# Convolution kernels of seven head groups: sum over n moved from TensorE to VectorE

## The chip, the cores and the metric

The kernel runs on one core of a Trainium2 chip. The metric is the device time of one launch in microseconds (us). Three runs of the kernel before gave 977.91, 977.95 and 978.32 us, so the median is 977.95 us. Of the core's engines this text uses TensorE (PE in the profile; its weight loads are the row PEld), VectorE (DVE), ScalarE (ACT), GpSimd (POOL) and the DMA queue that SyncE issues (SP).

## The reference

The input `x` has 64 batch entries, 64 heads h and 1024 positions l. Two layers are applied. The first is a masked long convolution with one kernel for each head, and the second a gated low-rank expert layer that is added to `x`:

```
A = -exp(log_A_real) + 1j*A_imag            # 64 heads x 64 n
dtA = A * exp(log_dt)
Cs = Cc * (exp(dtA) - 1) / A
K = 2 * real( sum over n of Cs[h,n] * exp(dtA[h,n] * l) )     # 64 x 1024
y = (causal convolution of x*mask with K) + x*mask*D[h],  times mask
scores = y @ Wr.T;  top 16 of 64 -> softmax -> gates G
out = x + 2 * einsum( (y @ A_experts) * G, B_experts )
```

What is changed here is one step in the first layer: how the sum over n is taken for the first 128 positions of K.

## The kernel before

**Groups.** The 64 heads are worked on in 8 groups of 8 heads (`HG`), a group being 4 pairs of heads (`GP`). The positions are cut into 8 blocks of 128 (`P`). For each group the generator `tables(g)` makes the tables of the convolution, `conv(g, ...)` computes `y` of the group, `gates(g, y)` the gates, and `first(g, ...)` the first half of the expert layer (`h` products, line L553, in a seven-product scheme for 2x2 blocks). When all groups are done, `second(...)` computes the other half (`s` products, L1042), from about 582 us on.

**Interleaving.** These pieces are generators. A group's `h` products are laid between the convolution steps of the next group and the table steps of the group after that, so that TensorE always has something to do. The order on each engine is made by a scheduler when the program is built; it orders by its own estimates wherever the code doesn't pin the order. Each engine then runs its instructions strictly in that order. An instruction whose input is late holds all that stands behind it on its engine.

**Tables of a group.** From `mag`, `sn`, `sh` comes `w` (L355, powers of exp(dtA) for 129 positions). For each pair i a table `b` of 128 partitions (2 heads x 64 n) by 128 positions is made twice: `b[:, 0, :]` is the real part, whose sum over n is the kernel K, and `b[:, 1, :]` the other part. Both are turned by TensorE (`transpose`, L326, into the PSUM tile `pb`) and copied by ScalarE to `bt` (L330). So `bt[:, i, P:]` holds the turned real part: positions on partitions, 2 heads x 64 n along the row. `bt` is the stationary operand of `pu` (L618), which makes the states `s` that are carried from block to block (`recur`, L366).

**The first chunk of K.** `kernels` (L285 and on) sums over n on TensorE: `heads` is a 128x2 constant with ones for each head's 64 rows, and `pk` = heads^T times `b[:, :, 0, :]` (L293), two matrix multiplications of 256 columns for a group from the second on. ScalarE copies `pk` to `ks` (L296), 2 partitions by 4 pairs by 128 positions. `rows` adds D to position 0 (VectorE, L355, `ks`), writes the rows to the DRAM buffer `krows` (L303) and reads them back as a Toeplitz matrix `toep` (L305): 128 partitions, each one position further on. `toep` is the stationary operand of `pc` (L644). The carried states are added into the same `pc` (L653), and VectorE masks it into `y` (L661).

**What stands around it.** `pb`, `pk`, `pu`, `psh`, `psc` and `pg` share two PSUM buffers (`ps_k`). `psh` and `psc` (L722, L731) are the scores of the group that has just finished its convolution; `pg` (L766) turns its gates. `ps_f` has four banks for `h`. `tabp` holds one buffer for each tag (`mag`, `f`, `k`, `sn`, `ks`); the second pair of `b` tables lies in the buffer with tag `k`, which the next group's `k` tile (L362) uses after it.

Of the kernel before, what the change touches and what calls it, by code (L numbers as in the profile page):

```python
# [37 lines left out]
F32 = mybir.dt.float32  # L38
I32 = mybir.dt.int32
AF = mybir.ActivationFunctionType  # L40
ALU = mybir.AluOpType
AX = mybir.AxisListType
PSUM = bass.MemoryType.PSUM

P = 128
# [9 lines left out]
HG = 8  # L55
NG = NH // HG
# [7 lines left out]
GP = HG // 2  # L64
NW = P + 1
NCH = NBLK - 1
KROW = P - 1 + P
# [22 lines left out]
    return c  # L90


def body(ctx: ExitStack, tc, x, xo, lens, par, dvec, at, bm, wt, cst, out):
    nc = tc.nc
    V = nc.vector
    G = nc.gpsimd
# [4 lines left out]
    def pool(stack, name, bufs, side, **kw):  # L101
        return stack.enter_context(tc.tile_pool(name=name, bufs=bufs, side=side, **kw))
# [5 lines left out]
    ps_k = psum.enter_context(tc.tile_pool(name="ps_k", bufs=2, space=PSUM))  # L108
# [7 lines left out]
    const = pool(right, "const", 1, "right")  # L116
    xp = pool(right, "xp", 4, "right")
    tp = pool(right, "tp", 1, "right")
    tabp = pool(right, "tabp", 1, "right")
# [8 lines left out]
    cst_sb = ids.tile([P, NW + P + 2 + NBLK], F32, tag="cst", name="cst_sb")  # L128
    nc.scalar.dma_start(cst_sb, cst)
    lens_sb = prep.tile([P, NB], I32, tag="lens", name="lens_sb")  # L130
    d_sb = const.tile([2, NP], F32, tag="dvec", name="d_sb")
    nc.scalar.dma_start(d_sb, dvec)
    lv = cst_sb[:, :NW]
    ident = cst_sb[:, NW : NW + P]
    heads = cst_sb[:, NW + P : NW + P + 2]
# [2 lines left out]
    krows = dram.tile([NH, KROW], F32, tag="krows", name="krows")  # L138
# [98 lines left out]
    def tables(g):  # L237

        j0 = g * GP
        wide = [P, GP, NW]

        def new(t, name=None):
            return tabp.tile(wide, F32, tag=t, name=f"{name or t}_{g}")

        mag, f, k = new("mag"), new("f"), new("k")
        for i in range(GP):
            nc.scalar.activation(mag[:, i, :], lv, AF.Exp, scale=dt_re[:, j0 + i : j0 + i + 1])
        tt(f, tu_hi[:, j0 : j0 + GP].unsqueeze(2).to_broadcast(wide),  # L250
           lv.unsqueeze(1).to_broadcast(wide), ALU.mult)
        yield
        ts(k, f, MAGIC, ALU.add, MAGIC, ALU.subtract)
        yield
        tt(f, f, k, ALU.subtract)
        yield
        for i in range(GP):
            stt(f[:, i, :], lv, tu_lo[:, j0 + i : j0 + i + 1], ALU.mult, f[:, i, :], ALU.add)
            if i % 2:
                yield  # L260
        ts(f, f, HALF_IN, ALU.min, -HALF_IN, ALU.max)

        sh, sn = new("k", "sh"), new("sn")
        nc.scalar.activation(sh, f, AF.Sin, scale=math.pi)
        nc.scalar.activation(sn, f, AF.Sin, scale=2.0 * math.pi)
        nc.scalar.activation(sh, sh, AF.Square)
        nc.scalar.activation(sh, sh, AF.Copy, scale=-2.0, bias=1.0)
        yield
        w = tab2.tile([P, 2, GP, NW], F32, tag="w", name=f"w_{g}")
        tt(w[:, 1], mag, sn, ALU.mult)  # L270
        yield
        tt(w[:, 0], mag, sh, ALU.mult)
        yield
        alpha, nbeta, nalpha = (scales[q] for q in ("alpha", "nbeta", "nalpha"))
        bt = tp.tile([P, GP, 2 * P], F32, tag="bt", name=f"bt_{g}")

        def others():
            return (tab2.tile([P, 3, GP], F32, tag="turn", name=f"turn_{g}"),
                    tp.tile([P, HG, P], F32, tag="toep", name=f"toep_{g}"))

        if g == 0:
            turn, toep = others()
            tabs[g] = (w, bt, turn, toep)
        h0 = g * HG
        all_rows = tabp.tile([2, GP, P], F32, tag="ks", name=f"ks_{g}")  # L285

        def kernels(bbs, i):


            n = i + 2 * len(bbs)  # L290
            pk = ps_k.tile([2, n - i, P], F32, tag="pk", name=f"pk_{g}_{i}")
            for m, bb in enumerate(bbs):
                nc.tensor.matmul(pk[:, 2 * m : 2 * m + 2, :], lhsT=heads, rhs=bb[:, :, 0, :],  # L293
                                 start=True, stop=True)
            ks = all_rows[:, i:n, :]
            nc.scalar.copy(ks, pk)  # L296
            return ks, i, n

        def rows(ks, i, n):

            tt(ks[:, :, 0], ks[:, :, 0], d_sb[:, j0 + i : j0 + n], ALU.add)
            row = krows[h0 + 2 * i : h0 + 2 * i + 1, :]
            nc.sync.dma_start(  # L303
                krows[h0 + 2 * i : h0 + 2 * n, P - 1 :].rearrange("(i a) l -> a i l", a=2), ks)
            nc.sync.dma_start(toep[:, 2 * i : 2 * n, :],  # L305
                              bass.AP(row.tensor, row.offset, [[1, P], [KROW, 2 * (n - i)], [1, P]]))

        bbs, halves = [], []
        for i in range(GP):
            j = j0 + i  # L310
            re, im = w[:, 0, i, :P], w[:, 1, i, :P]
            if i % 2 == 0:
                bb = tabp.tile([P, 2, 2, P], F32, tag=("sn", "k")[i // 2], name=f"b_{g}_{i}")
                bbs.append(bb)
            b = bb[:, i % 2]
            for c, by in enumerate((alpha, nbeta)):
                if g == 0:
                    ts(b[:, c, :], re, by[:, j : j + 1], ALU.mult)
                else:
                    nc.scalar.activation(b[:, c, :], re, AF.Copy, scale=by[:, j : j + 1])  # L320
            stt(b[:, 0, :], im, nbeta[:, j : j + 1], ALU.mult, b[:, 0, :], ALU.add)
            stt(b[:, 1, :], im, nalpha[:, j : j + 1], ALU.mult, b[:, 1, :], ALU.add)
            if g == 0 or i % 2 == 0:
                pb = ps_k.tile([P, 1 if g == 0 else 2, 2 * P], F32, tag="pk", name=f"pb_{g}_{i}")
            for c in range(2):
                nc.tensor.transpose(pb[:, i % 2 if g else 0, (1 - c) * P : (2 - c) * P], b[:, c, :], ident)  # L326
            if g == 0:
                nc.scalar.copy(bt[:, i, :], pb[:, 0])
            elif i % 2:
                nc.scalar.copy(bt[:, i - 1 : i + 1, :], pb)  # L330
            if g == 0 and i % 2:
                halves.append(kernels(bbs[i // 2 :], i - 1))
            if g == 0 and i == 3:
                rows(*halves[0])
            yield
        if g:
            turn, toep = others()
        V.tensor_copy(turn[:, 0:2], w[:, :, :, P])
        ts(turn[:, 2], turn[:, 1], -1.0, ALU.mult)
        if g == 0:  # L340
            yield
            rows(*halves[1])
            return
        ks = kernels(bbs, 0)
        yield
        rows(*ks)
        tabs[g] = (w, bt, turn, toep)


# [4 lines left out]
    def tt(o, a, b, o_):  # L354
        V.tensor_tensor(out=o, in0=a, in1=b, op=o_)  # L355
        return o

    def ts(o, a, s1, o1, s2=None, o2=None):
        if o2 is None:
            V.tensor_scalar(out=o, in0=a, scalar1=s1, scalar2=None, op0=o1)  # L360
        else:
            V.tensor_scalar(out=o, in0=a, scalar1=s1, scalar2=s2, op0=o1, op1=o2)  # L362
        return o

    def stt(o, a, s, o1, b, o2):
        V.scalar_tensor_tensor(out=o, in0=a, scalar=s, in1=b, op0=o1, op1=o2)  # L366
        return o
# [101 lines left out]
    marks = {}  # L469
    sums = factors_by_identity(*wa_quarters, wa)  # L470
    steps0 = tables(0)
    next(steps0)
    for _ in some(sums, 1):
# [625 lines left out]
    def steps_of(g):  # L1099
        return tables(g) if g < NG else iter(())  # L1100
# [21 lines left out]
    for g in range(NG):  # L1122
# [18 lines left out]
        if g == 0:  # L1141
            tables1, n = steps_of(1), 0
# [50 lines left out]
    n = 0  # L1193
    for _ in products:
# [3 lines left out]
        if n in (5, 6):  # L1198
            i = (1, 6)[n - 5]
# [77 lines left out]
```

## Time and profile before

The profiled execution took 978.31 us, of which 976.5 us are the span from the first to the last instruction.

| | busy us | share of the span | instructions |
|---|---|---|---|
| PE | 963.7 | 99% | 4312 |
| PE weight load | 723.8 | 74% | 4312 |
| DVE | 724.2 | 74% | 1682 |
| ACT | 159.7 | 16% | 310 |
| POOL | 334.8 | 34% | 285 |

One float32 product of TensorE shows as two matmul records (each L293 multiplication, for example), and one transpose as one record. The granted TensorE clock is full in all 40 slices of the span.

The profile names an instruction by the line of the code, the engine, the operation, and the tiles that it writes and reads. "Idle before" is the time for which an engine stood still ahead of an instruction, with what released it. A row of the timeline that ends in "x2" holds two instructions that follow one another. The chain of waits is followed back from the last instruction to what each step waited for; when an engine is in that chain with back-to-back work, a microsecond less of this work is a microsecond less of time, as long as nothing else is late.

### The profile page before, as it was taken

The numbers are of one execution on the slowest core, as the hardware profiler recorded it, in microseconds if no ns is written. First come the engines' busy times: TensorE is split into PE (matmuls) and PEld (weight loads), VectorE is DVE, ScalarE is ACT, GpSimd is POOL, SyncE is SP. The second block draws the span as 40 slices with busy tenths as digits, with TensorE's granted clock in tenths as the row PEclk, the third lists the DMA queues.
The fourth block names the chain that finished last, engine by engine and source line by source line (L and its number), as shares of the span: only waits on it lengthen the run. The fifth ranks groups of instructions, "written<-read, shape, count | busy, mean of one in ns | idle before, by whom it ended". The sixth has DMA issues, their size and how long they took to land.

```text
span 976.5 us, 11964 instructions
## 1 busy us (share of the span) xinstructions
PE 963.7 (99%) x4312; PEld 723.8 (74%) x4312; DVE 724.2 (74%) x1682; ACT 159.7 (16%) x310; POOL 334.8 (34%) x285
## 2 busy tenths in 40 slices
PE   7999999999999999999999999999999999999998
PEld 2476666676676686586676678888888888888887
DVE  8889798597687687686656769778966785686674
ACT  5344151230330221131101000000000000000000
POOL 0212112042023023132123112247545663754555
PEclk9999999999999999999999999999999999999999
DMA  7825234325325305315305254683674466267422
GB/s 281 226 56 167 70 119 141 108 89 155 109 75 159 114 36 158 139 55 157 140 23 167 77 178 162 198 300 105 216 260 132 168 209 231 90 214 266 134 108 108
DMA packets 67456, 143.99 MB, mean 147 GB/s; under 512 B 9478, under 2 KB 18246, under 8 KB 67398
## 3 DMA queue, kind: packets, MB, share of 16 engines
q1 hardware_dynamic: 49378, 94.40, 28.7%
q0 software_dynamic: 16864, 47.22, 15.1%
q10 hardware_dynamic: 1156, 1.61, 0.6%
q8 instruction: 34, 0.56, 0.2%
q14 instruction: 24, 0.20, 0.1%
HBM read 94.89 MB, written 47.25 MB: 146 GB/s over the span
## 4 chain that ended last, share of the span: by engine, by line
PE 93%; DVE 4%; DMA 1%; ACT 1%; issue 0%; POOL 0%; DVEq 0%
PE h L553 39%; PE s L1042 34%; PE pc L644 5%; PE pc L653 5%; PE pu L618 5%; PE psh L722 3%; PE pb L326 1%; PE pk L293 1%; DMA toep<-krows 1%; DMA krows<-ks 0%; PE last L1042 0%; PE pg L766 0%; DVE s L366 0%; PE psc L731 0%; DVE hg L355 0%
## 5 line engine op out<-in xcount | busy, mean ns | idle before, releaser
L366 DVE SCALAR_TENSOR_TENSOR s<-s,turn 128x128 f32<-128x128 f32 (+1 forms) x558 | 153.2, 321 | 26.5 <-ACT s L623 20.2
L553 PE MATMUL h<-y,waa 128*128 128x256 f32 x512 | 120.7, 383 | 0.0
L553 PE MATMUL h<-y,was 128*128 128x256 f32 x512 | 117.6, 381 | 0.0
L553 PE MATMUL h<-ty,was 128*128 128x256 f32 x512 | 116.8, 380 | 0.0
L553 PEld LDWEIGHTS h<-y,waa 128*128 128x128 f32 x512 | 94.4, 190 | 27.1 <-issue 15.3
L553 PEld LDWEIGHTS h<-y,was 128*128 128x128 f32 x512 | 96.0, 190 | 20.9 <-issue 7.2
L553 PEld LDWEIGHTS h<-ty,was 128*128 128x128 f32 x512 | 96.5, 190 | 17.5 <-issue 4.8
L804 POOL TENSOR_TENSOR hg<-h_p,gx 128x512 f32<-128x512 f32 x16 | 28.7, 1796 | 213.3 <-DVE h_p L366 210.3
L804 POOL TENSOR_TENSOR hg<-h_u,gx 128x512 f32<-128x512 f32 x32 | 48.9, 1528 | 112.1 <-DVE h_u L355 111.6
L661 DVE TENSOR_TENSOR y<-pc,mask 128x512 f32<-128x512 f32 x64 | 41.2, 684 | 44.1 <-PE pc L653 44.1
L1056 ACT COPY p<-s 128x512 f32<-128x512 f32 x28 | 16.4, 586 | 312.4 <-PE s L1042 312.4
L901 POOL TENSOR_TENSOR o<-o,acc_a 128x512 f32<-128x512 f32 x32 | 47.7, 1510 | 41.4 <-ACT acc_a L919 21.6
L644 PE MATMUL pc<-x,toep 128*128 128x512 f32 x128 | 60.0, 593 | 0.3 <-DMA toep<-krows 0.3
L553 PE MATMUL h<-ty,waa 128*128 128x256 f32 x256 | 58.6, 381 | 0.0
L777 POOL DMA_DIRECT2D gx<-gt_dram x56 | 33.6, 629 | 67.3 <-DMA gt_dram<-gt 67.3
L623 ACT COPY s<-pu 128x448 f32<-128x448 f32 x62 | 32.9, 532 | 144.3 <-PE pu L618 144.0
L618 PE MATMUL pu<-x,bt 128*64 128x448 f32 x256 | 55.1, 552 | 1.2 <-ACT gt L768 1.2
L553 PEld LDWEIGHTS h<-ty,waa 128*128 128x128 f32 x256 | 48.0, 190 | 9.9 <-issue 3.5
L653 PE MATMUL pc<-s,w 64*128 64x448 f32 x248 | 54.7, 561 | 0.0
L901 POOL TENSOR_TENSOR o<-o,b_room 128x512 f32<-128x512 f32 x32 | 49.2, 1557 | 9.8 <-DVE b_room L355 9.8
L355 DVE TENSOR_TENSOR o<-o,s 128x512 f32<-128x512 f32 x50 | 34.1, 682 | 23.0 <-PE s L1042 17.3
L355 DVE TENSOR_TENSOR hg<-hg 128x512 f32<-128x512 f32 x64 | 43.0, 684 | 9.5 <-POOL hg L804 8.8
(236 smaller groups left out, 1586.5 us busy)
## 6 DMA issues: line engine op xcount, KB each, us to landing
x<-in_x SPq DMA_DIRECT2D x32, 512.0 KB
hg_dram<-hg POOLq DMA_DIRECT2D x16, 1024.0 KB, 5.2
o<-in_xo SPq DMA_DIRECT2D x64, 256.0 KB
out<-o SPq DMA_DIRECT2D x63, 256.0 KB
gx<-gt_dram POOLq DMA_DIRECT2D x56, 256.0 KB, 6.1
qy<-hg_dram SPq DMA_DIRECT2D x28, 512.0 KB
r<-hg_dram SPq DMA_DIRECT2D x26, 512.0 KB
hg_dram<-hg POOLq DMA_DIRECT2D x16, 768.0 KB, 4.4
```

The lines of the kernel that those rows point to most:

```text
L355: V.tensor_tensor(out=o, in0=a, in1=b, op=o_)
L366: V.scalar_tensor_tensor(out=o, in0=a, scalar=s, in1=b, op0=o1, op1=o2)
L553: nc.tensor.matmul(bank[:, ii, :], lhsT=fac[n - 1][:, k, (j + ii) * P : (j + ii + 1) * P], rhs=rf[n - 1][:, k, :], start=(first and ii == ...
L618: nc.tensor.matmul(pu[hh * NS : (hh + 1) * NS, :], lhsT=bt[:, i, (1 - c) * P + hh * NS : (1 - c) * P + (hh + 1) * NS], rhs=xt[:, hh, : NCH ...
L623: marks["s"] = nc.scalar.copy(s[:, c], pu.rearrange("p (k b) -> p k b", b=NB))
L644: nc.tensor.matmul(pc, lhsT=toep[:, 2 * i + hh, :], rhs=xt[:, hh, :], start=True, stop=False)
L653: m = nc.tensor.matmul(pcs[hh][:, NB:], lhsT=w[o : o + NS, c, i, 1:], rhs=s[o : o + NS, c].rearrange("p k b -> p (k b)"), start=False, sto ...
L661: marks["y"] = V.tensor_tensor(out=y[:, :, i // 2, 2 * (i % 2) + hh, :], in0=pcs[hh].rearrange("p (k b) -> p k b", b=NB), in1=mask, op=ALU ...
L777: i = queue.dma_start(gx[:, ii, :], gt_dram[g, c * n : (c + 1) * n, :].unsqueeze(1).to_broadcast([n, RANK, TOK]),)
L804: G.tensor_tensor(out=o, in0=a, in1=b, op=op)
L901: tc.keep_in_program_order(G.tensor_tensor(out=o, in0=a, in1=b, op=op_))
L1042: nc.tensor.matmul(bank[:, ii, :], lhsT=left_[i - 1][:, k, ii * P : (ii + 1) * P], rhs=right_[i - 1][:, k, :], start=(first and ii == rows ...
```

## The change

For the groups 1 to 7 (group 0 keeps the old way) the two L293 multiplications of a group go. In their place VectorE sums over n along the rows of the turned tables: one `tensor_reduce` over `bt[:, :, P:]`, 128 partitions by 512 elements, gives `kc`, 128 positions by 8 heads. One TensorE transpose turns `kc` to `pk`, now 8 heads by 128 positions, ScalarE copies that to `ks8`, and VectorE adds D from a new small constant `d_of_group` (8 heads by 8 groups, one further DMA at the start on ScalarE's queue). One DMA writes the 8 rows of `krows`, and the DMA that makes `toep` is the same as before. The tag `ks` falls away: group 0's `ks` uses the buffer of tag `mag`.

```diff
+    d_of_group = const.tile([HG, NG], F32, tag="dgrp", name="d_of_group")
+    nc.scalar.dma_start(d_of_group, dgrp)
...
         h0 = g * HG
-        all_rows = tabp.tile([2, GP, P], F32, tag="ks", name=f"ks_{g}")
+        if g == 0:
+            all_rows = tabp.tile([2, GP, P], F32, tag="mag", name=f"ks_{g}")
...
+        def kernels_by_vector():
+
+            kc = tabp.tile([P, HG], F32, tag="kc", name=f"kc_{g}")
+            V.tensor_reduce(kc.rearrange("p (i a) -> p i a", a=2),
+                            bt[:, :, P:].rearrange("p i (a n) -> p i a n", a=2), AX.X, ALU.add)
+            pk = ps_k.tile([HG, P], F32, tag="pk", name=f"pk_{g}")
+            nc.tensor.transpose(pk, kc, ident)
+            ks = tabp.tile([HG, P], F32, tag="ks8", name=f"ks8_{g}")
+            nc.scalar.copy(ks, pk)
+            return ks
+
+        def rows_by_head(ks):
+
+            tt(ks[:, 0:1], ks[:, 0:1], d_of_group[:, g : g + 1], ALU.add)
+            row = krows[h0 : h0 + 1, :]
+            nc.sync.dma_start(krows[h0 : h0 + HG, P - 1 :], ks)
+            nc.sync.dma_start(toep, bass.AP(row.tensor, row.offset, [[1, P], [KROW, HG], [1, P]]))
...
-        ks = kernels(bbs, 0)
-        yield
-        rows(*ks)
+        ks = kernels_by_vector()
+        yield
+        rows_by_head(ks)
...
+        "dgrp": D.reshape(NG, HG).T,
```

The instruction order of the changed program differs from that before only from the tables of group 1 on. In the order that the scheduler wrote for the changed program, between the last `pb` transpose of a group and the `pk` transpose there stand more records of `h` than there stood ahead of the L293 products: 12 in group 2, 10 in groups 3 to 6, and 8 in group 7, where before there were 2. In group 1 there are 16, as before. On VectorE the `k` and `f` steps of the next tables stand ahead of the new reduction in groups 1 and 3 to 6, and `k` and one `ty` step (L355, 128x1024) in group 2.

More of the change, by code (lines that the diff above doesn't have):

```diff
@@ L90, in constants, with body @@
     return c
-def body(ctx: ExitStack, tc, x, xo, lens, par, dvec, at, bm, wt, cst, out):
+def body(ctx: ExitStack, tc, x, xo, lens, par, dvec, dgrp, at, bm, wt, cst, out):
     nc = tc.nc
```

## The prediction

> **What bounds the kernel.** I read first the busy table and the shares of the chain of waits, then the busy time by stage, then the timeline around the removed instruction. The chain says whose work sets the end, and the stages say where that holds:
>
> ```profile
> PE 93%; DVE 4%; DMA 1%; ACT 1%; issue 0%; POOL 0%; DVEq 0%
> ```
>
> ```profile
> 117.00:145.00 28.00, 26.26 (x121) 15.63 (x120) 24.81 (x73) 12.42 (x24) 4.74 (x7) 1.00 0.34 113
> 258.00:334.00 76.00, 76.00 (x340) 52.45 (x340) 55.95 (x157) 17.17 (x34) 17.50 (x18) 1.00 0.35 113
> ```
>
> In these two rows of the busy time by stage (length, then PE, PEld, DVE, ACT, POOL, clock, DMA) the second is the repeating stage of one group: TensorE is busy for all of its 76 us, VectorE for 56. There, TensorE work that is removed shortens the time one for one, unless something is late. The first row is the only stage of groups 1 to 7 that is different: TensorE stands for 1.74 us in 28, with VectorE at 89%. Seven sums are removed; on the chain of waits they stand near 74, 122, 186, 259, 335, 412 and 488 us. I call them groups 1 to 7. The timeline of a repeating group (start, duration, engine):
>
> ```profile
> 257.88 0.88 PE L326 MATMUL pb<-cst_sb,b 128*128 128x128 f32 x6
> 257.98 1.29 DVE L661 TENSOR_TENSOR y<-pc,mask 128x512 f32<-128x512 f32 x2 [2.66 <-PE pc L653]
> 258.36 1.07 ACT L330 COPY bt<-pb 128x512 f32<-128x512 f32 x2 [10.28 <-PE pb L326]
> 258.60 0.60 PE L553 MATMUL h<-y,waa 128*128 128x256 f32 x2
> 259.12 1.02 PE L293 MATMUL pk<-b,cst_sb 128*2 128x256 f32 x4
> 260.08 3.65 PE L722 MATMUL psh<-y,wt_sb 128*64 128x512 f32 x16
> 260.19 0.43 DVE L362 TENSOR_SCALAR k<-f 128x516 f32<-128x516 f32 x1 [0.92 <-PE pk L293]
> 260.65 0.69 DVE L355 TENSOR_TENSOR f<-f,k 128x516 f32<-128x516 f32 x1
> ```
>
> The reader is to see that TensorE goes from `pb` to `psh` without a gap; that `pk` holds it for 0.96 us (259.12 to 260.08); and that VectorE waits 0.92 us for `pk`, because `k` takes over a buffer that `pk` reads.
>
> **Removed and added TensorE work.** Four records go from each group, 0.96 us. One transpose comes. Six transposes of `pb` take 0.72 us (257.88 to 258.60), so one is 0.12 us. It can hide its weight load only if `kc` is there early; if TensorE waits for `kc`, I add 0.1 us for the load (a `pb` load is 0.14 us for 128 columns, a `pk` load 0.08 us for 2). So 0.84 us is saved where nothing waits, and 0.74 us less the wait elsewhere.
>
> **The new reduction.** No row has 512 elements to 8 in SBUF. The nearest are
>
> ```profile
> L733 DVE TENSOR_REDUCE sc<-psc 128x256 f32<-128x512 f32 x8 | 5.5, 690 | 11.6 <-PE psc L731 11.6
> L752 DVE TENSOR_REDUCE den<-sa 128x4 f32<-128x256 f32 x8 | 3.3, 414 | 0.1
> ```
>
> 690 ns for as many inputs from PSUM, 414 ns for half as many from SBUF. I take 0.68 us; the ends are 0.41 and 0.83 (twice L752). A rule speaks against this step: the Trainium skill ("VectorE: DVE Perf Modes", section "Rules for kernel authors") says of `tensor_reduce` on a hot path to expect the lowest speed, "it's the slowest DVE op. Consider restructuring". If VectorE bounded the groups, the sum would be 7 x 0.68 = 4.8 us slower. The rows say it doesn't: in the repeating stage VectorE idles 20 of 76 us, and 0.92 us of that lies exactly where the reduction goes, as `k` need no longer wait for `pk`. I follow the rows. What matters is whether `kc` comes before TensorE gets to its transpose.
>
> **Groups 3 to 6.** The order written for the changed program has on VectorE: y, y, k, f, reduction. From the rows: y starts at 257.98; the next instruction follows 1.20 us later (each y is spaced 0.60), so k at 259.18, f at 259.64 (0.46 after k, as now), the reduction at 260.25 (0.61 after f, as the 0.69 us operations are spaced), end 260.93; TensorE sees it 0.12 us later, as `psh` follows `y` now (y ends 123.06, `psh` loads at 123.18). `bt` is ready at 259.43. So `pk` can start at 261.05. TensorE has 10 records of h between `pb` and `pk` instead of 2. It now ends the two at 259.12; eight more at 0.216 us (16 records of a product span 3.45 us on the chain) give 260.85. It waits 0.2 us, loads and transposes for 0.22, and `psh` starts about 261.30. Today, with the same ten records done, it would be at 260.08 + 1.73 = 261.81. **Saved: 0.5 us each, 2.0 us for four.** Ends: 0.1 (reduction 0.83 us, and an operation held up by GpSimd) to 0.75. GpSimd stands still in this place (it waits 24.6 us until 275.5), so I keep 0.5. Behind `psh`, the scores come 0.8 us later on their own timeline; `pg` needs them at 287.7, the last gate operation ends at 274.8 now: 13 us of cover (5 us in group 3).
>
> **Group 7.** Reduction directly behind the two y: y starts at 486.81, reduction at 488.02, `pk` possible at 488.8; TensorE, with 8 records of h, gets there at 489.2. No wait: **0.8 us**.
>
> **Group 1.** 16 records of h (3.46 us) lie between `pb` and `pk`, as before. VectorE idles 3.42 us there; k, f, the reduction and the `f` steps fall into this hole, and the reduction ends about 72.4, before 74.0. **0.8 us.** What follows is the doubtful part: `w` (two) and the next `f` now stand among the recurrence, while GpSimd multiplies gates. What that costs is seen today:
>
> ```profile
> 76.47 3.81 DVE L366 SCALAR_TENSOR_TENSOR f<-cst_sb,p_tulo,f 128x129 f32<-128x129 f32 x3
> 77.53 2.60 POOL L804 TENSOR_TENSOR hg<-h_u,gx 128x512 f32<-128x512 f32 x2
> ```
>
> Three `f` steps that take 0.9 us elsewhere last 3.8. They move out of GpSimd's way, others move in. By hand the recurrence (36 steps, 0.22 us each) ends near 87.5 instead of 88.7, and is needed at 90.5 - 0.8. A hold as large as today's 2.9 us would be just late by 0.7 us: ends -0.5 and +0.85.
>
> **Group 2.** TensorE isn't the bound here. Order on VectorE: y, y, k, `ty`, reduction. From
>
> ```profile
> 121.78 1.28 DVE L661 TENSOR_TENSOR y<-pc,mask 128x512 f32<-128x512 f32 x2
> 123.10 1.22 DVE L355 TENSOR_TENSOR ty<-y 128x1024 f32<-128x1024 f32 x1
> 123.21 3.65 PE L722 MATMUL psh<-y,wt_sb 128*64 128x512 f32 x16 [0.58 <-DVE y L661]
> 139.94 0.56 ACT L768 COPY gt<-pg 64x512 f32<-64x512 f32 x1
> 140.56 0.97 PE L618 MATMUL pu<-x,bt 128*64 128x448 f32 x4 [1.16 <-ACT gt L768]
> ```
>
> y ends 123.06, k 0.36, `ty` 1.14, reduction 0.68: 125.2. TensorE has 12 records ahead and is there at 123.7: it waits 1.6 us, and `psh` starts at 125.5. Today, with the same work done, it would be at 123.21 + 10 x 0.216 = 125.4: even. Then ScalarE's sines and VectorE's `w` (0.6 each), `f` and two `b` steps stand ahead of the end of the gates. Stepping through: scores reduced 131.0 to 131.7, exp at 135.5, gates done 140.1, `pg` at 140.2 where TensorE comes at 138.6, `gt` copied by 141.3, `pu` without a wait (today 1.16 us). At the end of the first `pu` TensorE stands at 141.5 against 141.4 today with equal work. **-0.1 us**, ends -1.5 (a further table load of 1.28 us in the way) and +0.7.
>
> **The rest, at nothing.** The D addition is one small operation for another (0.15 us), the copy is 8x128 instead of 2x512, and ScalarE has room. `krows` gets 8 rows in one DMA as before, `toep` is the same DMA, and SyncE's queue keeps its order; `toep` lands at least 4 us ahead of `pc` in group 1 (issued 79.05, used 88.65) and 35 us in the others. The new constant's DMA takes some 0.5 us of ScalarE's queue at 1.7 us, and ScalarE waits until 3.5 us for `cst_sb` anyway. Group 0's `ks` in `mag`'s buffer makes group 1's `mag` (31.92 today) wait for a DMA that has landed by 31.94; ScalarE then idles 11 us.
>
> **Sum.** 0.8 - 0.1 + 2.0 + 0.8 = 3.5 us. The profiled execution took 978.31 us (976.5 of span and 1.8 around it), 0.36 above the median of the three runs, 977.95. So 974.8 by the one, 974.45 by the other; I say **974.6**. Its own range, from the ends above added with some cancelling, is 972.7 to 976.0. From no change a measurement tells about 0.2%, 2 us.
>
> **Rivals.** (a) *The wait takes the place of the work*: `kc` is late by 0.5 us more than I worked out in groups 3 to 6 and group 2 loses 0.7, or the time won is given back at 653 us, where TensorE waits for VectorE's sums of loaded factors with DMA at 82%. For it: my margin is 0.2 us, less than one VectorE operation. Against: GpSimd is still, and the factor loads are started by the same chain, so they shift too. Gain 3.5 - 2.0 - 0.7 = 0.8: 977.3, chance 0.22. (b) *The gates of group 2 become the bound* (the other side): table work that now precedes them on VectorE and ScalarE (two table loads of 1.28, two `w`, an `f`, two `b`, the reduction: 5.9 us in all, of which I found 1.6 to show at `pg`) shows in full, 4.3 us more, and `pu` waits for `gt` as today, 1.2 more: 977.95 - 3.5 + 5.5 = 980.0. It eats the gain from `pg` later than 143.7, and decides from about 145. For it: VectorE is at 89% there; against: most of it falls into waits for `psc` and for ScalarE. Chance of ending slower by 0.2%: 0.13. (c) *The change does nothing* since the `pk` time is a modelled figure: 0.96 us is read from start to start, so I leave this within (a).
>
> **How the numbers follow.** Main 0.65, (a) 0.22, (b) 0.13, and these are the chances of faster, same and slower. The range reaches from the good end, 972.6, to 978.0, which takes in (a) and leaves out (b) and a little below.
>
> **What would show it.** L293 with 4 records only; a `pk` transpose of 8x128 seven times, 0.12 us each; a reduction near 0.68 us; TensorE's wait for `kc` near 0.2 us in groups 3 to 6, 1.6 in group 2, none in 1 and 7; `pg` of group 2 near 140; repeating stages shorter by 0.5 us. Waits for `kc` above 0.7 us in the repeating groups, or `pg` beyond 143.7, would make the prediction wrong.

## The result and the profile after

The changed kernel takes **974.32 us** (median of 6 runs, 973.99 to 974.75), against 978.07 for the kernel before in the same session (6 runs, 977.91 to 978.32): a ratio of 0.9961 (95% interval 0.995 to 0.9973), 3.75 us less. The profiled execution took 974.48 us with a span of 972.7. The forecast was 974.6.

The busy row of the page of the changed kernel, and the shares of its chain of waits:

```profile
PE 959.6 (99%) x4291; PEld 722.5 (74%) x4291; DVE 726.1 (75%) x1689; ACT 157.3 (16%) x310; POOL 334.8 (34%) x285
...
PE 93%; DVE 4%; DMA 2%; issue 0%; ACT 0%; POOL 0%; SPq 0%; DVEq 0%
```

There are 21 matmul records fewer (seven groups, four out and one in), and seven VectorE instructions more. TensorE still sets the end. The busy time by stage of the changed kernel (length, then PE, PEld, DVE, ACT, POOL, clock, DMA), for the stage of group 2 and for one repeating group:

```profile
117.00:145.00 28.00, 25.91 (x119) 15.57 (x118) 24.28 (x74) 13.93 (x29) 4.72 (x7) 1.00 0.33 111
256.90:332.28 75.38, 75.31 (x337) 52.28 (x337) 56.50 (x158) 16.74 (x34) 17.53 (x18) 1.00 0.39 113
```

The repeating stage is 75.38 long where it was 76.00, and TensorE is as full as before. In group 2 TensorE still stands, 2.09 us of 28 (1.74 before). The timeline of the repeating group (group 4) in the changed kernel, whose lines lie 20 to 25 further on:

```profile
256.78 0.88 PE L348 MATMUL pb<-cst_sb,b 128*128 128x128 f32 x6
256.88 1.29 DVE L683 TENSOR_TENSOR y<-pc,mask 128x512 f32<-128x512 f32 x2 [2.66 <-PE pc L675]
257.26 1.07 ACT L352 COPY bt<-pb 128x512 f32<-128x512 f32 x2 [10.28 <-PE pb L348]
257.50 2.32 PE L575 MATMUL h<-y,waa 128*128 128x256 f32 x10
258.09 0.42 DVE L384 TENSOR_SCALAR k<-f 128x516 f32<-128x516 f32 x1
258.54 0.69 DVE L377 TENSOR_TENSOR f<-f,k 128x516 f32<-128x516 f32 x1
259.15 0.68 DVE L306 TENSOR_REDUCE kc<-bt 128x8 f32<-128x512 f32 x1
259.89 0.08 PEld L309 LDWEIGHTS pk<-cst_sb,kc 128*8 128x8 f32 x1 [0.47 <-DVE kc L306]
259.89 0.27 PE L309 MATMUL pk<-cst_sb,kc 128*8 128x128 f32 x1
260.09 1.08 PE L744 MATMUL psh<-y,wt_sb 128*64 128x512 f32 x4
```

The reduction takes 0.68 us and ends at 259.83. `k` follows `y` without the wait of 0.92 us that it had. TensorE's ten `h` records would end at 257.50 + 10 x 0.216 = 259.66, the transpose starts at 259.89, and `psh` 0.20 later.

To see where the time went I compare, between timelines, the starts of pieces of work ahead of which the same work has been done: the first `psh` (51.08 before), the first `pc` behind group 1 (88.65), the row of `h` behind group 2's first `pc` and `pu` (158.51), and `pg` of the later groups (211.67, 287.95, 364.22, 440.50, 516.78). The difference of two such starts is a group's time. Time gained on the kernel before, in us (negative is lost):

| kernel | group 1 | group 2 | groups 3 to 6, each | group 7 |
|---|---|---|---|---|
| predicted | 0.8 | -0.1 | 0.5 | 0.8 |
| changed kernel | 0.26 | 0.30 | 0.61 to 0.62 | 0.84 |
| e1, records put back | -0.70 | -0.61 | -0.34 to -0.39 | -0.14 |
| e2, k free (sums on TensorE) | -0.35 | 1.57 | 0.01, -4.14, -0.01, 0.01 | -0.04 |
| e9, e2 with one sine behind `gt` | -0.34 | 1.57 | -0.04 to 0.01 | -0.04 |
| e3, reduction doubled | 0.60 | 0.19 | 0.50 to 0.52 | 0.85 |
| e4, reduction first | 0.26 | 1.82 | 0.84 to 0.85 | 0.85 |
| e5, pu in a row | -1.48 | 0.29 | 0.61 to 0.62 | 0.85 |
| e6, e4 and e5 | -1.22 | 1.82 | 0.84 to 0.85 | 0.85 |
| e7, sines behind | 0.85 | 0.30 | 0.61 to 0.62 | 0.85 |
| e8, e4 and e7 | 0.85 | 1.82 | 0.84 to 0.85 | 0.85 |

The changed kernel's row adds to 3.86. Its first `psh` was 0.08 later than before, and from group 7 on the gain stays 3.78 to 3.79, so nothing is given back at 653 us.

### The profile page after: what moved, and what is told of

The parts are those of the page before. It is cut to its first block, busy times and chain, and to the rows that moved or that the text cites. A ratio compares the mean times of both kernels' runs of the same rounds, so it can differ in the third digit from the quotient of the medians.

```text
span 972.7 us, 11924 instructions
## 1 busy us (share of the span) xinstructions
PE 959.6 (99%) x4291; PEld 722.5 (74%) x4291; DVE 726.1 (75%) x1689; ACT 157.3 (16%) x310; POOL 334.8 (34%) x285
## 4 chain that ended last, share of the span: by engine, by line
PE 93%; DVE 4%; DMA 2%; issue 0%; ACT 0%; POOL 0%; SPq 0%; DVEq 0%
PE h L575 39%; PE s L1064 34%; PE pc L666 5%; PE pc L675 5%; PE pu L640 5%; PE psh L744 3%; PE sum L195 1%; DVE y L683 1%; DMA waa<-in_at 1%; DMA toep<-krows 1%; DMA krows<-ks 0%; DVE f L377 0%; PE pg L788 0%; DVE ty L377 0%; PE last L1064 0%; DVE s L388 0%
```

## The experiments

**e1: TensorE's records put back.** Is the gain TensorE's, or does it come from VectorE, which in groups 3 to 6 no longer stands 0.92 us for the sums?

```diff
-            pk = ps_k.tile([HG, P], F32, tag="pk", name=f"pk_{g}")
+            bank = ps_k.tile([HG, 3 * P], F32, tag="pk", name=f"pk_{g}")
+            pk = bank[:, :P]
             nc.tensor.transpose(pk, kc, ident)
+            for _ in range(2):
+                nc.tensor.matmul(bank[:2, P:], lhsT=heads, rhs=cst_sb[:, : 2 * P], start=True, stop=True)
```

> The changed kernel with two matmuls of 2 x 256 outputs (heads against constants, results read by nobody) put back behind each of the seven transposes: four TensorE records a group, as many as the change took away; VectorE keeps the new order. Theory (the gain is TensorE's records, one for one, where no other wait ends later): 7 x 0.96 = 6.7 slower than the changed kernel at most, and at least the 3.4 to 3.8 that the change gained; 978 to 981. Rival (the gain is that VectorE no longer stands 0.92 for the sums before k, and the records lay beside other work): stays at 974 to 975.

Measured: 981.05 us (980.99 to 981.4), ratio to the kernel before 1.0029 (1.0018 to 1.004), so 6.73 slower than the changed kernel. Group 4 of its timeline:

```profile
260.19 2.32 PE L578 MATMUL h<-y,waa 128*128 128x256 f32 x10
262.58 0.27 PE L310 MATMUL pk<-cst_sb,kc 128*8 128x128 f32 x1
262.79 1.02 PE L312 MATMUL pk<-cst_sb 128*2 128x256 f32 x4
263.74 3.65 PE L747 MATMUL psh<-y,wt_sb 128*64 128x512 f32 x16
```

The four records hold TensorE from 262.79 to 263.74, 0.95 us, and every group of the table loses 0.9 to 1.0 on the changed kernel. 7 x 0.96 = 6.7: these records of TensorE count one for one in all seven groups. (In group 2 TensorE waits for VectorE further on, but the records stand ahead of `psh`, from which the scores and the gates follow.)

**e2 and e9: only VectorE set free, in the kernel before.** The second pair of `b` tables gets a buffer of its own from group 1 on, so `k` has nothing to wait for; the sums stay on TensorE. The cut shows the main line; to make room, `ks` moves into the buffer of tag `sn` (in group 0, of `mag`).

```diff
-                bb = tabp.tile([P, 2, 2, P], F32, tag=("sn", "k")[i // 2], name=f"b_{g}_{i}")
+                bb = tabp.tile([P, 2, 2, P], F32, tag=("sn", "k" if g == 0 else "kb")[i // 2], name=f"b_{g}_{i}")
```

> The kernel before with only its buffers changed: k no longer takes the place of the second table that the summing matmuls read, so VectorE doesn't stand about 0.92 a group before k; the summing matmuls stay on TensorE. Theory (TensorE's records): TensorE's work and its waits in groups 3 to 6 are the same, 978 within 0.7. Rival (VectorE's freed stand is the gain): some 3.8 faster, 974.3.

Measured: 981.22 us (979.57 to 981.63), ratio 1.0029 (1.0017 to 1.0042). Both expectations missed: it is some 3 slower. The place is at 212 us, in the timeline of e2:

```profile
213.46 0.64 ACT L264 ACTIVATE sh<-f 128x516 f32<-128x516 f32 x1 [4.60 <-DVE f L363]
214.00 0.56 ACT L769 COPY gt<-pg 64x512 f32<-64x512 f32 x1
...
214.62 3.20 PE L619 MATMUL pu<-x,bt 128*64 128x448 f32 x8 [2.25 <-ACT gt L769]
```

With `k` free the scheduler runs the tables further ahead, and puts their sine in front of the copy of `gt`. The sine stands 4.60 us for `f`, `gt` stands behind it, and `pu` needs the buffer that `gt` empties: TensorE waits 2.25. More follows from this wait. The eight `pu` records behind it take 3.20 us where eight take 1.72 elsewhere, and the clock granted to TensorE is 0.52 in this stretch (the columns are those of the busy time by stage, the clock third from the end):

```profile
214.62:217.75 3.13, 3.13 (x9) 0.77 (x9) 0.72 (x3) 1.44 (x3) 0.00 (x0) 0.52 0.78 272
```

Five of the six executions of e2 have a mean clock of 0.998 and take 981.04 to 981.63 us; the sixth has 1.000 and takes 979.57. So about 1.6 us of e2's loss is the lower clock, and 2.25 the wait; group 2's gain of 1.57 (below) stands against them. e9 adds one order to e2, the sine behind that copy:

```diff
+        with tc.issue_after(marks["gt2"].ins) if g == 5 else ExitStack():
             nc.scalar.activation(sh, f, AF.Sin, scale=math.pi)
             nc.scalar.activation(sn, f, AF.Sin, scale=2.0 * math.pi)
```

> The kernel before with k's buffer freed, with one more order: the sine that stood 4.60 for its argument ahead of the copy of gt at 213 is issued behind that copy. TensorE's 2.25 wait and the records that it cut should go. Theory (the summing matmuls are still TensorE's, so groups 3 to 6 gain nothing; group 2 keeps the 1.6 that it gained when VectorE didn't stand 1.11 at 124.4): 976.5 within 0.5. Rival (the whole gain of the change is VectorE's freed stand): 974.3.

Measured: 976.98 us (976.85 to 977.21), ratio 0.9988 (0.9979 to 0.9997). That is within the theory's range, and the rival fell. The table says where: 1.57 gained in group 2, 0.34 lost in group 1, where `h` now cuts the row of `pu` once (see e7), and nothing in groups 3 to 7. In the repeating groups VectorE's stand of 0.92 us thus cost nothing: there the gain of the change is TensorE's alone.

The gain in group 2 has another cause than the one expected. VectorE had no stand of 1.11 us at 124.4 to lose: in the kernel before it was at work on `ty`, and `k` came in its turn. The chain of waits puts 1.11 us down to "issue" here, and that was misread as a wait:

```profile
124.36 1.23 DVE L355 TENSOR_TENSOR ty<-y,ty 128x1024 f32<-128x1024 f32 x1
125.50 0.15 DVE L355 TENSOR_TENSOR ks<-ks,d_sb 2x4 f32<-2x4 f32 x1
125.57 0.41 DVE L362 TENSOR_SCALAR k<-f 128x516 f32<-128x516 f32 x1
```

What moved is the table work. In e9 the `k` of these tables runs at 94.75 and their first sine at 98.65, where before they ran at 125.57 and 135.62. So the sines and the first `b` operations no longer stand on ScalarE between the gates and the copy of `gt`. TensorE's wait of 1.16 for `gt` is gone, and `h` cuts the row of `pu` once where it cut it twice:

```profile
137.99 1.72 PE L620 MATMUL pu<-x,bt 128*64 128x448 f32 x8
138.10 0.58 ACT L770 COPY gt<-pg 64x512 f32<-64x512 f32 x1 [3.75 <-PE pg L768]
```

With about 0.3 for a cut (measured below in group 1) these two make 1.5 of the 1.57.

**e3: the reduction doubled.** Sums over both halves of `bt`; the second half's sums are not used.

```diff
-            kc = tabp.tile([P, HG], F32, tag="kc", name=f"kc_{g}")
-            V.tensor_reduce(kc.rearrange("p (i a) -> p i a", a=2),
-                            bt[:, :, P:].rearrange("p i (a n) -> p i a n", a=2), AX.X, ALU.add)
+            kc = tabp.tile([P, 2 * HG], F32, tag="kc", name=f"kc_{g}")
+            V.tensor_reduce(kc.rearrange("p (c i a) -> p i c a", c=2, a=2),
+                            bt.rearrange("p i (c a n) -> p i c a n", c=2, a=2), AX.X, ALU.add)
...
-            nc.tensor.transpose(pk, kc, ident)
+            nc.tensor.transpose(pk, kc[:, HG:], ident)
```

> The changed kernel with each reduction made over both halves of the turned table, 1024 elements in the row where there were 512; only the half that is needed is turned to rows, the other half's sums are read by nobody. Each reduction should go from 0.68 to about 1.2. Theory (VectorE has room, TensorE only has to have enough rows of the chain ahead of the transpose): 0 to 1 slower, 974.3 to 975.3. Rival (the reduction lies on the path, so a slow operation is paid in full): 7 x 0.53 = 3.7 slower, 978.

Measured: 974.37 us (974.33 to 974.57), within 0.1 of the changed kernel. The rows of `kc` in e3 (duration minimum, median, maximum in ns) and of group 4's TensorE:

```profile
L306 DVE TENSOR_REDUCE kc<-bt x7: 1210/1212/1221, 71.5 to 485.2; 128x16 f32<-128x1024 f32 x7
```

```profile
257.08 2.75 PE L575 MATMUL h<-y,waa 128*128 128x256 f32 x12
260.00 0.27 PE L309 MATMUL pk<-cst_sb,kc 128*8 128x128 f32 x1 [0.17 <-DVE kc L306]
```

Each reduction is 0.53 longer, 3.7 in all. The scheduler answered by laying 12 `h` records ahead of the transpose where it had laid 10 (in group 2 14 for 12), and each of groups 2 to 6 lost only 0.1. Group 1 won 0.34 on the changed kernel, by another arrangement of `pu` (below), which with an earlier start hides the 0.5 in the total. The end of the reduction does lie on the path in these groups, since TensorE waits 0.17 for `kc`; but four fifths of the added time are covered by records laid ahead of the transpose. The rule that the prediction weighed (the Trainium skill, "VectorE: DVE Perf Modes", section "Rules for kernel authors") calls `tensor_reduce` on a hot path the slowest operation of VectorE and advises restructuring; here 3.7 us more of it cost 0.5 in the groups, because TensorE bounds them and VectorE has room.

**e4: the reduction first.** Two orders on VectorE: the next tables' `k` (those of groups 3 to 7) behind the reduction that stood after it, which is in groups 2 to 6, and the first `ty` step behind the reduction in group 2.

```diff
-        ts(k, f, MAGIC, ALU.add, MAGIC, ALU.subtract)
+        with tc.issue_after(marks["kc"].ins) if g > 2 else ExitStack():
+            ts(k, f, MAGIC, ALU.add, MAGIC, ALU.subtract)
...
-        tt(t1, b11, b12, ALU.subtract)
+        with tc.issue_after(marks["kc"].ins) if name == "ty1_" else ExitStack():
+            tt(t1, b11, b12, ALU.subtract)
```

> The changed kernel with the reduction issued on VectorE ahead of k in groups 3 to 7, and ahead of the y stage's first subtraction in group 2. Theory (in groups 3 to 6 TensorE waits 0.14 for the reduction, in group 2 1.35): 4 x 0.14 = 0.5 gained, plus 0 to 1.3 in group 2; 972.9 to 974. Rival (what TensorE waits for there is followed by another wait that ends as late, the gates in group 2 or the recurrence): 974.3 within 0.3.

Measured: **971.72 us** (971.65 to 971.75), ratio 0.9933 (0.9919 to 0.9946), 2.60 below the changed kernel and more than the theory's 1.8 at most. Group 2 in the timeline, first of the changed kernel, then of e4:

```profile
122.81 0.41 DVE L384 TENSOR_SCALAR k<-f 128x516 f32<-128x516 f32 x1
123.14 1.21 DVE L377 TENSOR_TENSOR ty<-y 128x1024 f32<-128x1024 f32 x1
124.27 0.67 DVE L306 TENSOR_REDUCE kc<-bt 128x8 f32<-128x512 f32 x1
...
125.00 0.27 PE L309 MATMUL pk<-cst_sb,kc 128*8 128x128 f32 x1 [1.35 <-DVE kc L306]
```

```profile
122.48 0.68 DVE L307 TENSOR_REDUCE kc<-bt 128x8 f32<-128x512 f32 x1
123.08 1.22 DVE L378 TENSOR_TENSOR ty<-y 128x1024 f32<-128x1024 f32 x1
...
123.21 0.27 PE L310 MATMUL pk<-cst_sb,kc 128*8 128x128 f32 x1 [0.74 <-DVE kc L307]
```

Measured from `y` (121.61 and 121.28), `k` and `ty` put the reduction 1.46 us later: it starts 2.66 behind `y` in the one and 1.20 in the other. `pk` comes as much earlier, TensorE has four records of `h` less ahead of it, and its later wait of 0.75 for `pg` is gone too. Group 2 gains 1.5 more than in the changed kernel, and each of groups 3 to 6 0.23 more. That is the wait read above (0.23 from 259.66 to 259.89), rather than the 0.14 that I had written. In groups 3 to 7 e4 has the full 0.84 or 0.85, which is 0.96 less 0.12.

**e5 and e6: group 1's `pu` in a row.** Group 1 gained 0.26 of 0.84. Its sixteen `pu` records are cut twice by `h` in the changed kernel:

```profile
74.16 0.97 PE L640 MATMUL pu<-x,bt 128*64 128x448 f32 x4
75.06 1.56 PE L575 MATMUL h<-y,waa 128*128 128x256 f32 x6
76.55 1.72 PE L640 MATMUL pu<-x,bt 128*64 128x448 f32 x8
78.21 0.70 PE L575 MATMUL h<-y,waa 128*128 128x256 f32 x2
78.83 0.97 PE L640 MATMUL pu<-x,bt 128*64 128x448 f32 x4
```

e5 forbids the cuts on TensorE (e6 is e4 and e5 together):

```diff
-        c11 = product(1, more=True)
+        with tc.issue_after(marks["pu"].ins) if (name, j) == ("h0", 2) else ExitStack():
+            c11 = product(1, more=True)
```

> The changed kernel with group 1's sixteen pu records in one row again, as in the kernel before: the first product of the h row that cut into them is issued behind the last. Theory (group 1 gained only 0.25 of 0.84 because each change between pu and h costs TensorE about 0.2): 0.58 faster, 973.7. Rival (group 1's gain was eaten by the recurrence, which ended 89.46[...], and by the wait for it behind the row): no change, 974.3 within 0.2.

> Both edits together: reduction first, and group 1's pu records in a row. If both theories hold, the sum of the two gains, 1.1 or more: 972.4 to 973.3. If only one holds, that one's time.

Measured: e5 975.79 us (975.31 to 976.23), ratio 0.9973 (0.9963 to 0.9983), 1.47 *slower* than the changed kernel; e6 973.51 (973.09 to 974.03), 1.79 slower than e4. Both theories missed. TensorE in e5:

```profile
73.86 2.58 PE L641 MATMUL pu<-x,bt 128*64 128x448 f32 x12
76.94 0.97 PE L641 MATMUL pu<-x,bt 128*64 128x448 f32 x4 [0.50 <-ACT s L646]
...
86.36 3.72 PE L575 MATMUL h<-y,waa 128*128 128x256 f32 x16 [1.34 <-ACT h_p L591]
```

Two waits for ScalarE take the place of the cuts: 0.50 for a `pu` buffer that it had not emptied, and 1.34 for its copy of `h`, which stood behind eight `b` operations, a table load and a `mag`. So the cuts were not to be had back by force: they filled time in which ScalarE was late.

**e7 and e8: what made ScalarE late.** ScalarE in group 1 of the changed kernel:

```profile
75.18 0.53 ACT L645 COPY s<-pu 128x448 f32<-128x448 f32 x1 [0.40 <-PE pu L640]
75.61 0.64 ACT L268 ACTIVATE sn<-f 128x516 f32<-128x516 f32 x1
76.14 0.62 ACT L269 ACTIVATE sh<-sh 128x516 f32<-128x516 f32 x1
77.57 0.53 ACT L645 COPY s<-pu 128x448 f32<-128x448 f32 x1 [0.81 <-PE pu L640]
78.00 0.64 ACT L270 ACTIVATE sh<-sh 128x516 f32<-128x516 f32 x1
78.53 0.53 ACT L645 COPY s<-pu 128x448 f32<-128x448 f32 x1
```

In the kernel before, `k` came behind `pk`, at 75.28. Free of that, VectorE does `k` at 70.70 and finishes `f` at 73.97, so the sines of the next tables start at 74.00 (81.57 before) and stand among the copies that empty `pu`. e7 puts them behind the fourth of these copies, in the changed kernel; e8 does the same in e4:

```diff
+        with tc.issue_after(marks["s1"].ins) if g == 2 else ExitStack():
             nc.scalar.activation(sh, f, AF.Sin, scale=math.pi)
             nc.scalar.activation(sn, f, AF.Sin, scale=2.0 * math.pi)
```

> The changed kernel with one pair of ScalarE's sines held back: those of the tables after group 1's are issued behind the copies of group 1's first four pu tiles, as they stood in the kernel before. Theory (the sines came forward with VectorE, so the pu tiles were emptied later and the sixteen pu records were cut by h; with the copies first they stand in a row, with no wait for a free tile or for the copy of h): 0.58 faster, 973.7. Rival (the tables that now come later are missed behind group 1, as a wait of pb or of the reduction in group 2): no change or slower, 974.3 to 976.

> The kernel with the reduction first (971.72) with the same hold of the sines. Theory: 0.58 faster, 971.1. Rival: 971.7 or slower.

Measured: e7 973.62 us (973.52 to 973.76), 0.70 below the changed kernel; e8 **971.30 us** (971.12 to 971.38), ratio 0.9929 (0.9917 to 0.9942), 0.42 below e4 (0.6 in the spans of the two profiled executions). e7 bears its theory out; e8 lies between its theory (971.1) and its rival (971.7), nearer to the theory. TensorE in e7:

```profile
73.64 0.27 PE L310 MATMUL pk<-cst_sb,kc 128*8 128x128 f32 x1
73.85 3.33 PE L641 MATMUL pu<-x,bt 128*64 128x448 f32 x16
77.11 3.72 PE L576 MATMUL h<-y,waa 128*128 128x256 f32 x16
```

Nothing waits, and group 1 gains 0.85, all of it. The same 16 `pu` and 48 `h` records, from the start of `pu` to the start of `pc`, took 13.72 us in e7 and 13.73 in the kernel before (no cut), 13.97 in e3 and 14.07 in e2 and e9 (one cut), and 14.31 to 14.32 in the changed kernel, e1 and e4 (two cuts). The two cuts are thus the 0.58 that group 1 lost, and the early sines are what led to the cuts. e8 is the fastest of all the kernels run, 6.8 us below the kernel before.

## Why the prediction was right, point by point

**The sum** was 3.5 us; 3.86 were gained by the groups. That it came so close is luck in part: group 1 was 0.54 too high, group 2 0.40 and groups 3 to 6 together 0.46 too low.

**Four records out, one in: right.** e1 puts them back and costs 6.73 for the 6.72 worked out. Group 7 gained 0.84 for 0.8 predicted, with no wait. The single transpose was mis-sized without harm: from its start to that of `psh` it takes 0.20 (486.22 to 486.42), not 0.12, but the `h` records ahead of it are left 0.09 sooner than they were left for the old sum (eight in 1.73 us, where two took 0.52).

**The reduction: right.** 0.673 to 0.687 us for an estimate of 0.68. That its time lies for the most part beside other work is shown by e3.

**Groups 3 to 6: right mechanism, 0.61 for 0.5.** The end of `kc` was right to the hundredth (2.95 us behind the start of `y`). The term that was too large is what follows it: the forecast gave 0.12 until TensorE sees `kc` and 0.22 for the load and the transpose, together 0.34; from 259.83 to 260.09 it is 0.26.

**Group 2: 0.30 for -0.1.** Measured from the start of `y`, `psh` came after 3.60 us (forecast 3.72) and `pg` after 17.70 (18.42), with waits of 1.35 and 0.75 where 1.6 and 1.6 were forecast. So the step from `psh` through the gates was forecast 0.6 too slow, and this is the term that was mis-sized. That `pu` no longer waits for `gt` was right. TensorE's waits in this stage grew from 0.58 and 1.16 to 1.35 and 0.75, 0.36 in all, which leaves 0.48 of the 0.84; 0.30 were measured, and the rest stays open. In e4, where 0.74 is the only wait, the same sum gives 1.84, and 1.82 were measured. Rival (b), the gates as the bound, fell: `pg` is far from 143.7. But it had a real place, as the wait of 0.75 for the gates and e4 and e9 show. One reading of the prediction was off: the sum at 122 is not on the chain of waits, which runs over VectorE there from 117 to 134.

**Group 1: the term that was furthest off, 0.26 for 0.8.** The doubt was put in the right group and in the wrong place. I watched the recurrence on VectorE: it ended at 89.46 (forecast 87.5), with `w`, `f` and an `s` step held at 1.64, 1.76 and 1.35 us while GpSimd worked (0.69, 0.69 and 0.35 elsewhere), and was still in time for the `pc` at 90.28. The loss came over ScalarE, which the forecast counted as having room: its sines came 7.6 us earlier and met the copies of `pu`. e7 shows it: one order on ScalarE brings back 0.59, all that was missing.

**Rival (a), a wait in place of the work,** fell in the repeating groups: TensorE's stand there is 0.23. It did happen in e2 and e5, where one engine was set free or one order forced.

## What to carry to other kernels

Price removed work on the engine that is full for a whole stage, one for one, and then look at what each *other* engine does with the time it gets: here the freedom of `k` alone was worth 1.57 us in one stage, where it took the sines out of ScalarE's way to `gt`, nothing in the repeating ones, and in group 1 it brought the sines forward into the copies that TensorE needed. When such an order costs time, repair it on the engine that comes too early (e7), not on the one that waits (e5). A new producer that TensorE waits for belongs ahead of the work that nobody waits for: moving five reductions up by two VectorE operations each brought 2.6 us together, two thirds of what the change itself brought.

## What was not expected of the hardware

A cut of the `pu` records by a few `h` records costs TensorE about 0.24 to 0.34 us even where nothing waits (13.72, 13.97 to 14.07 and 14.31 us for none, one and two cuts). Which part of a cut costs this (the weight loads of two different shapes, or the first record after a change) no run here tells apart. VectorE's reduction grew from 0.68 to 1.21 us as the elements in a row grew from 512 to 1024, so 0.53 us for 512 elements and, by an estimate from these two sizes, 0.15 for the rest.

A wait can cost more than its length. Behind e2's stand of 2.25 us TensorE was granted about half its clock (0.52) for 3.1 us, in five executions of six by their mean clock, and eight records took 3.20 us for 1.72. Behind the stands of 1.34 and 1.35 us in e5 and in the changed kernel the granted clock stayed at 1.00. What decides this, no run here shows.
